# Reloading a residual in the layout of turned column tiles: four strided loads a tile, or an early DRAM-to-DRAM copy and one load

## The chip, the cores and the metric

The kernel runs on one core of one Trainium2 chip. The metric is device time in microseconds (us) of one execution, lower is better. In what follows PE is the matrix engine (PEld its weight loads), DVE the vector engine, ACT the scalar engine, POOL GpSimd, and SP the engine that here does nothing but issue transfers. SP and ACT each have a queue of transfers. All transfers are carried out by the same 16 DMA engines.

## The reference, cut to what matters

`x` has 3327 rows of 512 floats, `adj` is a 3327 x 3327 matrix, all in float32. There are two layers, each with a residual:

```python
# layer 0
h = maximum(layernorm(x), 0)
q, k, v = h @ Wq.T + bq, h @ Wk.T + bk, h @ Wv.T + bv
x = x + softmax(q @ k.T * scale + adj + adj) @ v
# layer 1
h = maximum(layernorm(x), 0)
A2 = adj + eye
dscale = diagonal(A2) ** -0.5
x = x + relu((dscale[:, None] * A2 * dscale[None, :]) @ (A2 @ h @ W.T))
```

The `x` between the two layers is called x1 in the kernel. It is computed in the middle of the program, and wanted again at the end, when `relu(...)` of layer 1 is added to it.

## The kernel before, in words

Rows are padded to 3328, which is 26 tiles of 128. They are split into two strips, `s = 0` and `s = 1`, each with two halves `y` of `HT[s]` = 7 or 6 row tiles, so `H[s]` is 896 or 768 rows. A first part computes the attention weights and leaves them in DRAM. Then come three big matrix products, numbered `g` = 0 (attention times h), 1 (A2 times h) and 2 (A2 times the result of 1 times W).

Each `g` is made of seven smaller products `ORDER = ("p5", "p1", "p6", "p7", "p2", "p3", "p4")` of a Strassen-like scheme, each for both strips, and each in seven **steps** (six pairs of row tiles and one single one). So one `g` has 7 x 2 x 7 = 98 steps. A step with a pair makes 14 matmul instructions at L918; a single one makes 8 at L909. `number_of(g, r, s, t)` is a step's number, and `run(k)` issues the program of step `k`.

Which work stands in which step is written out by hand: `at(k, what)` puts a function into the dictionary `between`, and the engines' instruction order is then fixed as traced (`in_order`, SP and DVE among them). In `run(k)` the order on SP is: the left tiles of step `k + 3` (`steps[k + 3].load()`, L832 and L836, two transfers of 448 or 384 KB into a ring of five slots, `a_ring`), then every function of `between[k]` that has "load" in its name, in the order in which it was registered. Those of the right-hand rows (`Right.load`, L856 and L870) are registered before the ones of this case. The sums that DVE makes of a left tile (`four_sums`, L163 to L165, behind L899 for a diagonal) are traced two steps ahead of the matmuls that use them, and DVE also combines finished products (`Gather`, L962 to L981).

The result of `g = 2` is held transposed, as column tiles `cts[s][y][d]` (128 features by `H[s]` rows). Twelve blocks at the very end are turned by PE (`turn_last`, `finish`). The other fourteen column tiles are handled by class `Columns`, one every three steps of the last three products: DVE turns the tile in 32 x 32 blocks (`turn`, L1145), scales it (`scale`, L1151), and adds x1 (`add`, L1154), and SP stores it to `out`, four transfers a tile (L1157, posted so that SP issues them two steps later). The x1 for this has to lie in the same block-turned layout. `load` (L1141) therefore fetches it from `x1d`, which is x1 row by row in DRAM, with four transfers of 32 partitions, whose contiguous runs are 32 floats or 128 bytes:

```python
rows = rows.rearrange("(j r) (c a e) -> c a r j e", r=32, a=4, e=32)
return [(tile[32 * a : 32 * a + 32].rearrange("r (j e) -> r j e", e=32), rows[self.d, a]) for a in range(4)]
```

The tile that receives it is one of two slots (`xp_slots`). The load is placed two steps ahead of `turn`, and four ahead of `add`. x1 itself is written by ACT's queue at the end of `g = 0` and in the beginning of `g = 1`, between 999 and 1218 us.

Of the kernel before, what the change touches and what calls it, by code (L numbers as in the profile page):

```python
# [10 lines left out]
F32 = mybir.dt.float32  # L11
# [4 lines left out]
P = 128  # L16
# [23 lines left out]
H = tuple(n * P for n in HT)  # L40
# [7 lines left out]
def graph_layers_kernel(  # L48
# [30 lines left out]
    nc = tc.nc  # L79
    NP, D = x.shape  # L80
    DC = D // P
# [13 lines left out]
    def half(k, shape, name):  # L95
        return arena.tile(shape, F32, name=name, tag=f"half{k}")
# [31 lines left out]
    dram = ctx.enter_context(tc.tile_pool(name="dram", bufs=1, space=bass.MemoryType.DRAM))  # L128
# [25 lines left out]
    pd = [[dram.tile([P, len(E_AT), H[s]], F32, name=f"p{s}_{t}") for t in range(HALF)] for s in range(2)]  # L154
    sumd = [[dram.tile([P, len(SUMS), H[s]], F32, name=f"sum{s}_{t}") for t in range(HALF)] for s in range(2)]
    x1d = [[dram.tile([HT[s] * P, D], F32, name=f"x1d{s}{y}") for y in range(2)] for s in range(2)]
    rowd = [[dram.tile([P, D], F32, name=f"row{g}_{i}") for i in range(NT)] for g in range(3)]
    normd = {k: [dram.tile([1, 2 * 4 * P], F32, name=f"norm{m}_{k}") for m in range(2)] for k in range(4)}
    t2d = [[dram.tile([P, 4, P], F32, name=f"t2{g}_{t}") for t in range(PAIRS + 1)] for g in range(3)]
# [157 lines left out]
    def after(ins, other):  # L317

        tc.add_manual_dep(ins.ins, other.ins.name,
                          mybir.DependencyInfo(mybir.DependencyClass.NoSync, mybir.DependencyReason.DATA),  # L320
                          reason="in_order")

    class Turned:
# [23 lines left out]
        def load(self):  # L347
            k, w = self.k, self.w
            self.other = half(2, [P, 2, BW], "a21")[:, :, :w]
            a11, a12, a22 = hp[k][:, 0], hp[k][:, 1], hp[k][:, 2]  # L350
            for y, blocks in enumerate(((a11, a12), (self.other, a22))):
                c0 = ROW[y * HALF + PACKS[k][0]] * P
                xs = xT[:, c0 : c0 + w].rearrange("(z c p) e -> z p c e", z=2, p=P)
                for z, to in enumerate(blocks):
                    after(nc.sync.dma_start(to, xs[z]), self.row)
            self.norms = []
            for m in range(2):
                self.norms.append(half(m, [P, 2, BW], "norms")[:, :, :w])
                self.loaded = nc.sync.dma_start(
                    self.norms[m], normd[k][m][0:1, : 2 * w].rearrange("a (y e) -> a y e", y=2).to_broadcast([P, 2, w]))  # L360
# [766 lines left out]
    class Columns:  # L1127
# [5 lines left out]
        def parts(self, tile, rows):  # L1133

            rows = rows.rearrange("(j r) (c a e) -> c a r j e", r=32, a=4, e=32)
            return [(tile[32 * a : 32 * a + 32].rearrange("r (j e) -> r j e", e=32), rows[self.d, a]) for a in range(4)]

        def load(self):
            self.x = next(xp_slots)()[:, : H[self.s]]
            for to, rows in self.parts(self.x, x1d[self.s][self.y]):  # L1140
                nc.sync.dma_start(to, rows)  # L1141

        def turn(self):
            self.o = turn_ring([P, H[0]], "turned")[:, : H[self.s]]
# [20 lines left out]
    def number_of(g, r, s, t):  # L1165
        return ((g * len(ORDER) + r) * 2 + s) * len(every) + t

    def at(k, what, *args):
        between.setdefault(k, []).append((what, args))
# [44 lines left out]
    for n, (s, y, d) in enumerate(((0, 1, 2), (0, 1, 3), (1, 1, 2), (1, 1, 3), (0, 0, 0), (0, 0, 1), (1, 0, 0),  # L1214
                                   (1, 0, 1), (0, 0, 2), (0, 0, 3), (1, 0, 2), (1, 0, 3), (0, 1, 0), (0, 1, 1))):
        part = Columns(s, y, d)
        for what, later in ((part.load, -2), (part.turn, 0), (part.scale, 1), (part.add, 2)):
            at(k + later, what)
        k += 3 if n < 12 else 2
    for n, i in enumerate(range(20, NT, 2)):  # L1220
        at(number_of(2, 6, 1, 2) + n, last_load, i)
# [494 lines left out]
```

## Time and profile before

| what | value |
|---|---|
| median of 3 runs | 2166.07 us (2165.14 to 2173.19) |
| the profiled execution's own time | 2169.72 us |
| its span from first to last instruction | 2167.9 us |
| PE busy | 2142.5 us (99%) |
| DVE busy | 1653.3 us (76%) |
| HBM read, written | 416.68 MB, 167.84 MB |
| DMA packets, those under 512 bytes | 400530, 139788 |
| the four loads of a tile, L1141 | 56 transfers of 112 or 96 KB, 1943.2 to 2135.2 us |
| the four stores of a tile, L1157 | 56 transfers, 1977.0 to 2156.1 us |

How to read it: times inside the profile count from the first instruction, so the profiled execution's 2169.72 us is its span and 1.8 us around it. PE is busy nearly always, so what counts is where it isn't. A row of the timeline or of the chain has a start, a duration, an engine and a line; a small q behind an engine's name means its sequencer, which waits and issues but doesn't compute. `a<-b` means that a is written from b. In a table of windows, each engine has its busy time and its number of instructions, then come the granted PE clock as a share, the mean busy share of the 16 DMA engines and what they moved in GB/s. That share adds the times of packets, which overlap, and can go above 1.

In this profile, the steps of `g = 2` begin at 1748 us, the last three products and with them the column tiles' loads at 1943 us.

### The profile page before, as it was taken

What the parts mean: (1) busy time and instruction counts of PE and PEld (TensorE: products, weight loads), DVE (VectorE), ACT (ScalarE), POOL (GpSimd) and SP (SyncE); (2) the same over time, 40 slices, a digit from 0 to 9 for tenths busy, and PEclk for the clock granted to TensorE, in tenths of its full rate; (3) what the DMA queues carried; (4) which work ended last, traced back from release to release, by engine and by line L of the source; (5) the groups of instructions that cost most, each with busy time, mean ns of one, the idle gap of its engine ahead of it and who ended that gap; (6) DMA issues with size and microseconds to landing.
All of it is one profiled execution on the core that took longest, in us unless ns stands there. A gap on an engine that the chain in (4) does not pass through costs nothing.

```text
span 2167.9 us, 20907 instructions
## 1 busy us (share of the span) xinstructions
PE 2142.5 (99%) x6272; PEld 1182.1 (55%) x6272; DVE 1653.3 (76%) x3235; ACT 273.1 (13%) x441; POOL 68.4 (3%) x63
## 2 busy tenths in 40 slices
PE   9999999999999999999999999999999999999997
PEld 5555555555555555555454555555666655555553
DVE  7479888888887688767777778886666568779886
ACT  5312211112110000001110000010111100000000
POOL 2000000000004000000111000000000000000000
PEclk9999999999999999999999999999999999999998
DMA  8678888888999899889797889886646368769997
GB/s 298 214 255 287 308 313 279 303 296 304 322 299 308 299 364 329 280 290 314 259 318 257 303 292 362 309 302 213 206 133 224 129 195 294 247 183 237 263 254 172
DMA packets 400530, 586.07 MB, mean 270 GB/s; under 512 B 139788, under 2 KB 273304, under 8 KB 400408
## 3 DMA queue, kind: packets, MB, share of 16 engines
q1 hardware_dynamic: 372472, 527.08, 74.5%
q10 hardware_dynamic: 27936, 57.56, 7.2%
q8 instruction: 52, 0.85, 0.2%
q14 instruction: 70, 0.57, 0.1%
HBM read 416.68 MB, written 167.84 MB: 270 GB/s over the span
## 4 chain that ended last, share of the span: by engine, by line
PE 90%; DVE 5%; DMA 3%; issue 1%; SPq 0%; POOL 0%; ACT 0%; DVEq 0%
PE p L918 52%; PE Y L541 13%; PE Z L541 6%; PE p L909 5%; PE p L1025 4%; PE pw L1086 3%; PE X L541 3%; PE Y L397 2%; PE Z L397 1%; DMA part<-in_adjT_dram 1%; DVE part L163 1%; DMA part<-p 1%; DMA rows<-row 0%; PE X L397 0%; DMA wk<-in_wk_dram 0%
## 5 line engine op out<-in xcount | busy, mean ns | idle before, releaser
L918 PE MATMUL p<-part,b 128*128 128x448 f32 (+1 forms) x3528 | 1261.2, 514 | 5.2 <-DVE part L962 4.0
L918 PEld LDWEIGHTS p<-part,b 128*128 128x128 f32 x3528 | 670.8, 190 | 549.4 <-issue 292.4
L163 DVE TENSOR_TENSOR part<-part 128x896 f32<-128x896 f32 (+1 forms) x252 | 257.0, 1020 | 79.0 <-DMA part<-sum 27.9
L541 PE MATMUL Y<-qt,hp 128*128 128x448 f32 (+1 forms) x832 | 308.2, 513 | 2.5 <-DVE g L553 1.6
L541 PEld LDWEIGHTS Y<-qt,hp 128*128 128x128 f32 x832 | 157.8, 190 | 136.2 <-issue 72.7
L541 PE MATMUL Z<-qt,hp 128*128 128x384 f32 (+1 forms) x416 | 162.2, 512 | 0.0
L165 DVE TENSOR_TENSOR part<-part,part 128x448 f32<-128x448 f32 (+1 forms) x219 | 129.5, 591 | 14.9
L164 DVE TENSOR_TENSOR part<-part,part 128x448 f32<-128x448 f32 (+1 forms) x219 | 129.4, 591 | 7.2
L909 PE MATMUL p<-part,b 128*128 128x448 f32 (+1 forms) x336 | 124.2, 512 | 0.0
L541 PEld LDWEIGHTS Z<-qt,hp 128*128 128x128 f32 x416 | 79.0, 190 | 66.2 <-issue 38.1
L545 DVE SCALAR_TENSOR_TENSOR g<-g,Y 128x384 f32<-128x384 f32 (+1 forms) x156 | 91.5, 586 | 29.7 <-PE Y L541 26.0
L961 ACT COPY part<-p 128x384 f32<-128x384 f32 (+1 forms) x33 | 16.6, 503 | 664.0 <-PE p L918 512.2
L909 PEld LDWEIGHTS p<-part,b 128*128 128x128 f32 x336 | 63.8, 190 | 54.1 <-issue 31.5
L548 ACT ACTIVATE g<-g 128x768 f32<-128x768 f32 (+1 forms) x48 | 43.0, 896 | 346.8 <-DVE g L545 286.9
L541 PE MATMUL X<-qt,hp 128*128 128x384 f32 (+1 forms) x208 | 81.1, 512 | 0.0
L962 DVE TENSOR_TENSOR part<-p,part 128x384 f32<-128x384 f32 (+1 forms) x33 | 19.3, 586 | 57.3 <-PE p L918 56.5
L1025 PE MATMUL p<-w,ct 128*128 128x512 f32 x136 | 61.6, 592 | 0.0
L541 PEld LDWEIGHTS X<-qt,hp 128*128 128x128 f32 x208 | 39.5, 190 | 33.1 <-issue 19.3
L981 DVE TENSOR_TENSOR ct<-p,part 128x448 f32<-128x448 f32 (+1 forms) x72 | 42.5, 609 | 18.2 <-PE p L909 13.8
L190 POOL TENSOR_TENSOR rstd<-ve,mhalf 128x1 f32<-128x1 f32 x46 | 38.7, 843 | 531.1 <-DVE ve L188 502.8
L1086 PE MATMUL pw<-w,rows 128*128 128x256 f32 x208 | 53.5, 380 | 0.4 <-DVE rows L1076 0.4
L1016 DVE TENSOR_TENSOR job<-job 128x896 f32<-128x896 f32 (+1 forms) x52 | 53.0, 1019 | 0.0
(194 smaller groups left out, 1683.2 us busy)
## 6 DMA issues: line engine op xcount, KB each, us to landing
part<-sum SPq DMA_DIRECT2D x104, 448.0 KB, 5.0
part<-p SPq DMA_DIRECT2D x91, 448.0 KB, 6.0
part<-sum SPq DMA_DIRECT2D x104, 384.0 KB, 3.8
part<-p SPq DMA_DIRECT2D x91, 384.0 KB, 4.6
part<-in_adjT_dram SPq DMA_DIRECT2D x78, 448.0 KB, 4.9
b<-row SPq DMA_DIRECT2D x234, 128.0 KB, 4.9
part<-in_adjT_dram SPq DMA_DIRECT2D x78, 384.0 KB, 3.7
g<-in_adjT_dram SPq DMA_DIRECT2D x52, 448.0 KB, 4.2
```

The costliest lines, as they stand in the source:

```text
L163: yield nc.vector.tensor_add(o[:, 0:2], g[:, 0:4:3], g[:, 1:2].to_broadcast([P, 2, g.shape[-1]]))
L164: yield nc.vector.tensor_add(o[:, 2], o[:, 1], g[:, 0])
L165: yield nc.vector.tensor_add(o[:, 3], o[:, 2], g[:, 2])
L397: nc.tensor.matmul(ps[:, :w], M[B[name]][:, c, o * P : (o + 1) * P], hp[k][:, A[name], c], start=start and c == 0, stop=c == 1, skip_group ...
L541: nc.tensor.matmul(ps[:, :wd], h_of(self.t, name, k), qt[B[name]][:, k], start=start and k == 0, stop=k == 1, skip_group_check=True)
L545: nc.vector.scalar_tensor_tensor(a[n], a[n], 2.0, ps[:, :wd], op0=ALU.mult, op1=ALU.add if sign > 0 else ALU.subtract)
L548: nc.scalar.activation(g[1], g[1], AF.Exp, **({"bias": pad} if self.t == HALF - 1 else {}))
L909: yield nc.tensor.matmul(ps[("p2", "p3", "p4", "p8")[k]][:, :w], b[:, z], a[:, 0, y], start=k == 3 and not self.seeded, stop=True, skip_gr ...
L918: yield nc.tensor.matmul(ps[r][:, :w], b[:, i], m, start=self.t == 0 and not adds, stop=self.t == PAIRS - 1 and r in ("p1", "p5", "p6", "p ...
L1016: nc.vector.tensor_add(self.a, self.a, self.b)
L1025: nc.tensor.matmul(ps, cts[s][y][d][:, k * P : (k + 1) * P], w[d], start=d == 0, stop=d == DC - 1)
L1086: nc.tensor.matmul(ps, a, W[B[name]][:, c], start=new and c == 0, stop=c == 1, skip_group_check=True)
```

## The change

x1 gets a second copy in DRAM, `x1c`, in the layout of the column tiles: for every `d`, 128 rows of `H[s]` contiguous floats. A new function `reload` writes a quarter of a tile into it, DRAM to DRAM, with one transfer on SP. Fourteen tiles make 56 quarters, which are put into steps 1 to 55 of `g = 2`, one a step (two in step 48), in the first four products. `load` then fetches a tile in one transfer. Its place in the order stays, and so do `turn`, `scale`, `add` and the stores. As "reload" has "load" in its name, `run(k)` issues it with the loads at the beginning of a step, behind those of the right-hand rows.

```diff
     x1d = [[dram.tile([HT[s] * P, D], F32, name=f"x1d{s}{y}") for y in range(2)] for s in range(2)]
+    x1c = [[dram.tile([DC, P, H[s]], F32, name=f"x1c{s}{y}") for y in range(2)] for s in range(2)]
...
+        def reload(self, a):
+
+            tile = x1c[self.s][self.y][self.d]
+            to, rows = self.parts(tile, x1d[self.s][self.y])[a]
+            nc.sync.dma_start(to, rows)
+
         def load(self):
             self.x = next(xp_slots)()[:, : H[self.s]]
-            for to, rows in self.parts(self.x, x1d[self.s][self.y]):
-                nc.sync.dma_start(to, rows)
+            nc.sync.dma_start(self.x, x1c[self.s][self.y][self.d])
...
         part = Columns(s, y, d)
         for what, later in ((part.load, -2), (part.turn, 0), (part.scale, 1), (part.add, 2)):
             at(k + later, what)
+        for a in range(4):
+            at(number_of(2, 0, 0, 0) + 1 + 4 * n + a - (n > 11), part.reload, a)
         k += 3 if n < 12 else 2
```

## The prediction

> **What bounds the kernel now.** The page comes first. PE is busy 2142.5 of 2167.9 us, so no change of transfers can bring more than PE's idle time and what a lowered clock costs it.
>
> ```profile
> PE 2142.5 (99%) x6272; PEld 1182.1 (55%) x6272; DVE 1653.3 (76%) x3235; ACT 273.1 (13%) x441; POOL 68.4 (3%) x63
> ```
>
> Second, the table of windows, for the two stages that the change touches (the first four products of g = 2, then the last three) and for the one place where PE stands still.
>
> ```profile
> 1748.00:1943.00 195.00, 195.00 (x561) 106.21 (x560) 146.20 (x274) 8.90 (x18) 0.00 (x0) 1.00 0.72 237
> 1943.00:2140.00 197.00, 192.25 (x542) 103.85 (x541) 163.08 (x280) 13.73 (x27) 0.00 (x0) 0.98 1.00 249
> 2107.50:2121.46 13.96, 9.21 (x24) 4.10 (x23) 7.12 (x10) 1.08 (x2) 0.00 (x0) 0.95 0.92 208
> 2121.46:2128.80 7.34, 7.34 (x14) 4.09 (x15) 7.19 (x13) 0.00 (x0) 0.00 (x0) 0.62 1.22 261
> ```
>
> The first stage has a full PE and a DMA share of 0.72. The second has a share of 1.00, and loses 4.75 us of PE, all of it after 2107.5. There the chain of waits leaves PE:
>
> ```profile
> 2081.87 20.31 PE p L918 x54
> 2102.18 0.51 SPq L836
> ...
> 2102.74 5.03 DMA part<-in_adjT_dram
> ...
> 2109.69 2.54 PE p L918 x6
> 2112.23 0.47 SPq L836
> ...
> 2112.80 5.74 DMA part<-in_adjT_dram
> ...
> 2121.46 15.26 PE p L918 x38
> ```
>
> Two left tiles come late, and behind each hang DVE's sums and then PE: 0.76 us at 2109 and 3.98 us at 2117.5 by the timeline of PE. Why they are late is in the timeline of SP (start, duration):
>
> ```profile
> 2088.95 6.50 SPq L1141 DMA_DIRECT2D part<-x1d  x4
> 2095.55 0.94 SPq L836 DMA_DIRECT2D part<-in_adjT_dram  x2
> ...
> 2097.49 4.58 SPq L1157 DMA_DIRECT2D out_dram<-turned  x4
> 2102.17 1.68 SPq L836 DMA_DIRECT2D part<-in_adjT_dram  x3
> 2103.95 8.18 SPq L1141 DMA_DIRECT2D part<-x1d  x4
> 2112.23 0.94 SPq L836 DMA_DIRECT2D part<-in_adjT_dram  x2
> ```
>
> SP hands out the left tiles the moment it is through with a column tile's four loads. It was inside those for 8.18 us, 5.3 of them a wait for an earlier x1d load to land (SP's own waits), while a slot of the left ring had long been free.
>
> **What the Trainium skill says.** "DMA: Bandwidth & Descriptors", section "Why small descriptors are slow (HBM only)": each packet has a fixed cost. The trace agrees: in 1973 to 1976 us nothing but 128-byte loads ran, 1420 packets at a share of 0.377, so 0.377 x 3 us x 16 / 1420 = **12.7 ns** each; in 2147 to 2151 nothing but 128-byte stores, 3536 at 0.719, **13.0 ns** each. Same page, "Issuing engines are not separate DMA queues": all queues share the 16 engines, so an early copy has to fit beside that stage's own traffic. Same page, "Latency and other measured facts", gives the only price of DRAM to DRAM: 207 to 214 GB/s for tiles of 16 KiB rows. 128 bytes at that rate are an estimated 16 x 128 / 207 = 9.9 ns of one engine, below the fixed cost. No transfer here goes from DRAM to DRAM, so the trace doesn't say. "TensorE: Matmul & The Clock Gate", section "What's actually happening": after an idle window of about 3.4 us the clock is halved. The trace agrees: after 3.98 us idle the next 7.34 us had a clock of 0.62.
>
> **The change part by part.**
>
> *Taken away in the last three products:* 56 loads with 8 x 3584 + 6 x 3072 = 47104 packets, 47104 x 13 ns / 16 = 38 us of the DMA engines; and on SP the time inside them. The five tiles from 2070 on cost SP 5.63 + 6.50 + 8.18 + 5.11 + 3.61 = 29.0 us by its timeline.
>
> *Put in their place:* 14 loads of 448 or 384 KB in rows of 3584 or 3072 bytes, the shape of the left tiles (an issue 0.5 us, landing 4 to 5 us). 6.03 MB at the 349 GB/s of the best 20 us (1820 to 1840) are 17 us. So the stage gets 38 - 17 = 21 us of DMA back, about a tenth, and SP about 26 us from 2070 on. The stores stay, four small ones a tile, about 4.5 us of SP each.
>
> *The path:* with SP ahead again, left tiles are issued when their slot is free. The first of the two was 0.93 us late for DVE, the second 6.1. PE gets back 0.76 + 3.98 us, and 14 matmuls that took 7.34 us at the lowered clock take 4.51 (84 of this width take 27.09 elsewhere in the chain), 2.83 less. Sum **-7.6 us**. Late next is DVE: in this product it has about 5.3 us of work in a step of 5.26 us (its L163 start at 2084.0, 2089.3 and 2094.65, back to back), so its lead before PE stays near nothing but doesn't turn negative; between 2111 and 2121 it has 6.1 us of idle time that goes too. From PE's last L909 matmul at 2154.1 to the end, 13.8 us of combining, turning and storing stay as they are. Nothing more is to be had between 1943 and 2100, where PE is full.
>
> *The two waits of DVE* at 2136 to 2143 (0.2 and 3.64 us) lie after that; they vanish behind PE, which bounds the end then. I count nothing for them.
>
> *Added in the first four products:* 56 copies on SP, one a step. Issue: L1141's median is 0.605 us, so 34 us; at the price inside a group of four (some 5 us / 4) 70 us. This is hidden, since SP waits there for PE to free slots, 62.2 + 52.5 us in SP's own waits. Behind a copy on SP stands only the next step's left tile, which has to wait for PE anyway.
>
> ```profile
> SPq L832 <- PE p L918: 62.2, 33, 4.6
> SPq L836 <- PE p L918: 52.5, 22, 4.9
> ```
>
> Carrying: 47104 packets. At 13 ns 38 us, which with 0.72 x 195 = 140 us make 178 of 195: it fits, 0.7 us a step. The tightest part, 1800 to 1840, has a share of 0.95 and would go to about 1.13, 5 us late at its end. What covers that: a left tile is issued when PE leaves the step five before its own, so it has four steps of 4.5 to 5.3 us, at least 18 us; landing takes 5, the sums 1.09 + 0.62 + 0.63 = 2.3, and DVE's block of combining some 4.6. About 6 us are left. Bounds of the unknown price: below, 10 ns (the estimate above) or 28 us, no gain on the path since PE is full there; above, both ends in DRAM could add up to 26 ns or twice that. Free time in the stage is 0.28 x 195 = 55 us, used up at 55 x 16 / 47104 = 19 ns; with the 6 us of cover at 21 ns. I take 13 ns, since loads and stores, with DRAM on different sides, cost the same. Cost 0, range 0 to 25 us.
>
> *Waits added:* a load waits for its tile's copies, which were issued at least 37 steps before (the last tile: copied in steps 52 to 55, loaded in 92), some 170 us. If the wait covers the whole `x1c[s][y]`, the first load, in step 54, waits for a copy of the step before, which lands meanwhile. Nothing.
>
> The profiled 2169.72 becomes 2162.1, -0.35%. It lay 3.65 us above the median; the same 7.6 us off the median of 2166.07 give 2158.5, said as **2159**. A measurement tells about 0.5% here, 10.8 us, from no change, so this likeliest case is "within".
>
> **The rivals.**
>
> *A, half the gain (the end turns out bound by DVE, or by the stores):* DVE is 9.76 of 10 us busy from 2080 on, and stores still make SP stand 4 to 5 us a tile. Then the second stall shrinks under the length that lowers the clock but stays: -3 to -5, **2162**. For it: leads of near nothing. Against: DVE idles 6.1 us on a transfer right there.
>
> *B, slower: DRAM to DRAM is dear.* Place: steps of p1 and p6, 1800 to 1860, then to 1943. It decides from 21 ns a packet on; at 30 ns the copies are 88 us, 88 - 55 - 6 = 27 us of PE stall, less 7.6, so +19, **2185**; shorter stalls also lower the clock. For it: no row shows the price, and short writes to DRAM may each read first. Against: 128-byte stores to DRAM take the same 13.0 ns as loads from it.
>
> *C, the change doesn't take the wait away:* the left tile is late because of the stores, and the loads' time just goes to them. **2166**. Against: SP's longest stay, 8.18 us, is in L1141.
>
> *D, more than asked:* the unprofiled runs stall more, or the tail of 13.8 us shortens by 3 us with the DMA engines free: **2153**.
>
> **How the numbers follow.** Main case 0.50 (own range 2155 to 2163), A 0.15, C 0.06, D 0.11, B 0.18. Faster by over 0.5% (under 2155.2): D and the lower edge of the main case, 0.15. Slower by over 0.5% (over 2176.9): nearly all of B, 0.17. Within: 0.68. The range leaves out the far ends of D and B: 2152 to 2179.
>
> **What would show it.** Right: PE without a gap over 0.3 us from 1943 until its last L909, clock 1.00 there, SP's L1141 at 14 issues of about 0.5 us, left tiles never waited for at 2118, packets under 512 bytes unchanged in number but moved to 1748 to 1943, whose DMA share goes to about 0.92. Wrong: PE gaps behind L163 between 1800 and 1943, left tiles there landing over 8 us after their issue, copies of over 20 ns a packet; or the stall at 2117 still there with SP in L1157.

## The result, and the profile after

The changed kernel takes 2159.2 us in the median of 6 runs (2156.64 to 2160.37), the kernel before 2167.32 us in 6 runs, the three of the table above among them. The ratio is **0.9959, with a 95% interval of 0.9946 to 0.9972**. That is 8 to 9 us faster, as forecast (2159). It is less than the 0.5% that the prediction took a measurement to tell, but the interval lies clear of 1. The profiled execution took 2159.13 us, its span is 2157.3 us.

Lines of kernel.py move with the change: L918 is L919, L836 is L837, L909 is L910, L1104 is L1105; the copy is L1143, the one load of a tile L1147, its stores L1163. From the page of the changed kernel, and from its table of windows for the two stages and the place of the old gap:

```profile
PE 2137.5 (99%) x6272; PEld 1180.9 (55%) x6272; DVE 1652.0 (77%) x3235; ACT 273.1 (13%) x441; POOL 68.1 (3%) x63
```

```profile
1748.00:1943.00 195.00, 195.00 (x560) 106.21 (x559) 145.80 (x272) 8.61 (x17) 0.00 (x0) 1.00 0.86 261
1943.00:2140.00 197.00, 197.00 (x566) 107.35 (x565) 168.08 (x288) 14.20 (x28) 0.00 (x0) 1.00 0.87 255
...
2107.00:2121.00 14.00, 14.00 (x41) 7.60 (x40) 11.46 (x19) 1.08 (x2) 0.00 (x0) 1.00 0.79 232
```

PE is full in both stages, at full clock. The DMA share went from 0.72 to 0.86 in the first and from 1.00 to 0.87 in the second. The chain of waits no longer leaves PE in the last product, until 5.8 us before its last matmul ends:

```profile
2080.48 31.57 PE p L919 x84
2112.05 3.01 PE p L910 x8
2115.06 23.88 PE p L919 x74
```

Where the 10.6 us of span come from, by comparing the two profiles: 1.4 us lie ahead of the last product (it starts at 2081.87 before, at 2080.48 after). They are there from the 81st matmul on (25.09 us before, 23.70 after), which the change doesn't touch; in the profiles of all kernels of this document it starts between 23.55 and 25.09. From the start of the last product's matmuls to the end of the last L909 or L910 it is 2154.12 - 2081.87 = 72.25 us before and 2144.73 - 2080.48 = 64.25 after, so **8.0 us**. The tail behind that went from 13.8 to 12.6 us.

One correction to what stands ahead of the prediction: the steps of g = 2 begin earlier than 1748 us, since the weight products stand in its first steps. The copies run from 1671.4 to 1946.4 us. Of the 56, 44 lie in the stage from 1748 to 1943, one behind it, and 11 ahead of it, where DMA had more room (the packets of queue q1 at 45.6% of 16 engines between 1671 and 1748, against 33.8% before).

The price of a copy's packet, which no row of before could show, follows from the tables of DMA queues for 1748 to 1943, before and after:

```profile
DMA packets 21991, 46.12 MB, mean 237 GB/s; under 512 B 2433, under 2 KB 9221, under 8 KB 21982
...
q1 hardware_dynamic: 20686, 43.78, 68.3%
```

```profile
DMA packets 58576, 50.87 MB, mean 261 GB/s; under 512 B 38976, under 2 KB 45760, under 8 KB 58567
...
q1 hardware_dynamic: 57271, 48.53, 83.0%
```

36543 more packets under 512 bytes took 14.7% of 195 us on 16 engines, so 0.147 x 195 us x 16 / 36543 = **12.6 ns** each. From DRAM to DRAM costs what the loads (12.7) and the stores (13.0) of this size cost.

### The profile page after: what moved, and what is told of

Its sections match the earlier page's. It is cut to its first block, busy times and chain, and to the rows that moved or that the text cites. A ratio compares the mean times of both kernels' runs of the same rounds, so it can differ in the third digit from the quotient of the medians.

```text
span 2157.3 us, 20906 instructions
## 1 busy us (share of the span) xinstructions
PE 2137.5 (99%) x6272; PEld 1180.9 (55%) x6272; DVE 1652.0 (77%) x3235; ACT 273.1 (13%) x441; POOL 68.1 (3%) x63
## 4 chain that ended last, share of the span: by engine, by line
PE 93%; DVE 4%; DMA 2%; issue 1%; POOL 0%; ACT 0%; SPq 0%; DVEq 0%
PE p L919 55%; PE Y L542 13%; PE Z L542 6%; PE p L910 5%; PE p L1026 4%; PE pw L1087 3%; PE X L542 3%; PE Y L398 2%; PE Z L398 1%; DMA rows<-row 1%; DMA part<-sum 1%; PE X L398 0%; DMA wk<-in_wk_dram 0%; DVE part L164 0%; DVE st L185 0%
## 5 line engine op out<-in xcount | busy, mean ns | idle before, releaser
L919 PE MATMUL p<-part,b 128*128 128x448 f32 (+1 forms) x3528 | 1257.6, 513 | 0.8 <-DVE part L165 0.6
L919 PEld LDWEIGHTS p<-part,b 128*128 128x128 f32 x3528 | 669.9, 190 | 542.1 <-issue 291.8
L165 DVE TENSOR_TENSOR part<-part,part 128x448 f32<-128x448 f32 (+1 forms) x219 | 129.4, 591 | 7.2
L910 PE MATMUL p<-part,b 128*128 128x448 f32 (+1 forms) x336 | 124.2, 512 | 0.0
L910 PEld LDWEIGHTS p<-part,b 128*128 128x128 f32 x336 | 63.8, 190 | 54.1 <-issue 31.0
L963 DVE TENSOR_TENSOR part<-p,part 128x384 f32<-128x384 f32 (+1 forms) x33 | 19.3, 585 | 62.2 <-PE p L919 61.4
```

Of the source, the lines that this page charges most:

```text
L165: yield nc.vector.tensor_add(o[:, 2], o[:, 1], g[:, 0])
L910: yield nc.tensor.matmul(ps[("p2", "p3", "p4", "p8")[k]][:, :w], b[:, z], a[:, 0, y], start=k == 3 and not self.seeded, stop=True, skip_gr ...
L919: yield nc.tensor.matmul(ps[r][:, :w], b[:, i], m, start=self.t == 0 and not adds, stop=self.t == PAIRS - 1 and r in ("p1", "p5", "p6", "p ...
```

## The experiments

Theory S is the prediction's: SP is held inside four strided loads, so left tiles are issued late. Theory D: the DMA engines are overloaded in the last products, and taking small packets out is what helps. Theory X came up on the way. A completion semaphore is the counter that tells that a transfer has landed. SP may only issue a transfer when the one that used its completion semaphore before has landed; the semaphores go round among the transfers of SP and ACT in program order; and ACT issues its six loads of x1 for the last twelve blocks (L1104) late, when PE lets it. The traces bear the first two parts out: they name the semaphore of every transfer, and eight of them serve SP and ACT together, in turn. All ratios are to the kernel before on the same chip, with 95% intervals.

### Are the copies hidden?

**Copies made, but not used.**

```diff
-            nc.sync.dma_start(self.x, x1c[self.s][self.y][self.d])
+            for to, rows in self.parts(self.x, x1d[self.s][self.y]):
+                nc.sync.dma_start(to, rows)
```

> The 56 copies are made as in the change, but the tiles are still loaded with four 128-byte-run transfers from the rows. Theory S (the gain is SP's: it is no longer held inside four loads, and the copies are hidden): as before, ratio 0.998 to 1.002, about 2167 us, with PE's gap of some 4 us near 2117 still there. Theory C (the copies cost something, and the change's gain is net of it): slower than before by that cost, 2 us or more, and PE gaps between 1670 and 1950.

Measured: 1.0013 (1.0001 to 1.0025). PE is busy 195.00 of 195 us in the stage of the copies. The gap after 2117 is there (5.43 us), and one of 1.01 us at 2085. So the copies stall nothing where they run, but without the one load they bring nothing. The small loss sits in the last product; why it is a little larger there than before was not settled.

**Each copy made twice, and three times**, the further ones into DRAM tiles that nobody reads.

```diff
             nc.sync.dma_start(to, rows)
+            for other in spare_x1:
+                nc.sync.dma_start(self.parts(other[self.s][self.y][self.d], x1d[self.s][self.y])[a][0], rows)
```

> The change, with every copy made twice, the second into a DRAM tile that nobody reads: 112 copies, 94208 packets, an estimated 76 us of the DMA engines, as if one copy had 25 ns a packet. The prediction's sum (55 us free in the stage and 6 us of cover) gives 76 - 61 = 15 us of PE stall: 2174 us, ratio to before 1.003. Rival: the cover is larger, since part of the copies lies ahead of the stage counted and packets' times overlap: no PE gap, 2159 us, ratio 0.996.

> The change with every copy made three times, two of them into DRAM tiles that nobody reads: 168 copies, 141312 packets. Twice cost about 8 us of PE time in the stage of the copies (gaps of 4.9 us in all and two drops of the clock), while the gap at 2117 was gone. If the free time of the DMA engines is used up by then, every further packet costs in full: 44 of 56 copies lie in the stage, 44/56 x 38 = 30 us more, 2190 to 2200 us, ratio 1.010 to 1.014. If SP's waits for completions rather than the engines' time are what stalls: less, 2175 to 2185 us, 1.003 to 1.008.

Measured: twice 0.9994 (0.9984 to 1.0004), 2168.37 us; three times 1.0198 (1.0182 to 1.0213), 2211.26 us. Windows of the two, the stage of the copies:

```profile
1748.00:1943.00 195.00, 190.09 (x529) 101.12 (x528) 138.59 (x258) 8.52 (x17) 0.00 (x0) 0.98 0.98 274
```

```profile
1748.00:1943.00 195.00, 168.61 (x445) 87.67 (x444) 114.82 (x223) 5.95 (x12) 0.00 (x0) 0.92 0.98 252
```

Against the changed kernel (2159.2) that is 9.2 and 52.1 us (by the ratios 7.6 and 52). Twice lies between the two expectations, three times beyond both. The prediction's sum, copies less 55 us of free DMA time and 6 of cover, gives 76 - 61 = 15 and 115 - 61 = 54. It is too dear by 6 us or more at twice. That it fits at three times is in part luck: it counts all copies as lying in the stage, and it counts no lowered clock. Up to the last product's end PE idles for 32.6 us there, and 25.3 us of its matmuls ran at half the clock, an estimated 13 us more; some 5 us were not settled. At a DMA share of 0.98 PE pays in both kernels: at three times DVE's sums wait 58.2 us for left tiles (L163 of before, L165 here; its waits from 1748 to 1980). One set of copies, at a share of 0.86, cost PE nothing.

### What holds SP?

**The four strided loads spread**, one a step, no copy.

```diff
-            for to, rows in self.parts(self.x, x1d[self.s][self.y]):
-                nc.sync.dma_start(to, rows)
+            self.load_part(0)
...
+        for a in range(1, 4):
+            at(k - 2 + a, part.load_part, a)
```

> No copy and no second layout: the four strided loads of a tile are issued one a step, in the steps k-2 to k+1, instead of four in step k-2. Packets, bytes and stage are those of before. Theory S (SP's burst is what makes left tiles late): as the change, about 2159 us, ratio 0.996, PE without a gap after 1700. Theory D (what counts is the 21 us of DMA time that the change takes out of the last three products): stays at about 2167 us, ratio 0.999 to 1.001, left tiles still late at 2117.

Measured: 1.0021 (1.0011 to 1.0030), slower. Timeline of PE (start, duration, what, idle time ahead of it and who ended it):

```profile
2080.21 2.73 PE L918 MATMUL p<-part,b 128*128 128x448 f32 x6 [0.59 <-DVE part L962]
2085.62 25.07 PE L918 MATMUL p<-part,b 128*128 128x448 f32 x66 [2.69 <-ACT p L955]
2111.58 4.78 PE L918 MATMUL p<-part,b 128*128 128x448 f32 x12 [0.88 <-DVE part L164]
...
2123.74 29.77 PE L918 MATMUL p<-part,b 128*128 128x384 f32 x84 [4.38 <-DVE part L962]
```

The gap near 2117 stayed, and gaps at 2080 to 2086 came. An issue now takes 0.43 us in the median instead of 0.605, all 56 together 32.7 us of SP instead of 59.8, and still nothing is gained. **Theory S falls in the form that the prediction gave it**: to break up the burst is not enough. As a part of the cause the burst isn't out, since the tie of theory X is in this kernel too: SP waits 6.0 us between its loads of 2105.26 and 2111.72 us, with ACT's six loads of x1 just ahead in the round of semaphores. Spread loads without that tie were not run.

**The four strided loads on ACT's queue.**

```diff
-                nc.sync.dma_start(to, rows)
+                nc.scalar.dma_start(to, rows)
```

> Before, with the four strided loads of a tile issued in one burst as before, but from ACT's queue instead of SP's. Packets, bytes and burst stay. Theory S: SP is free, so about 2159 to 2161 us, ratio 0.996 to 0.997; the share of DMA in the last three products stays about 1.00. Theory D: about 2167 us, ratio 1.000, since the DMA engines carry the same.

Measured: 0.9994 (0.9985 to 1.0003). The gap near 2117 is gone, but PE now stands 0.74 us at 2020, 1.06 us at 2083.5 and 2.69 us at 2088.9. Between 2070 and 2140 SP, which no longer issues these loads, waits 20.2 us for them to land, although what it issues then are other tiles:

```profile
SPq L836 <- DMA part<-x1d: 13.1, 3, 4.7
SPq L856 <- DMA part<-x1d: 6.0, 2, 4.5
...
SPq L870 <- DMA part<-x1d: 1.1, 1, 1.1
```

So a transfer that ACT issued holds up those of SP. This is where theory X comes from. It also means that SP was not freed by this edit, so it is no clean test of theory S.

**The copies late**, one a step, seven to four steps ahead of the tile's load.

```diff
-            at(number_of(2, 0, 0, 0) + 1 + 4 * n + a - (n > 11), part.reload, a)
+            at(k - 9 + a, part.reload, a)
```

> The change, with each tile's four copies made one a step in the steps k-9 to k-6, seven to four steps ahead of its load, so inside the last three products. SP issues there 5 transfers a tile, never in a burst of four loads, but the DMA engines carry the 38 us of small packets in that stage again, and the 17 us of long ones on top. Theory D (the DMA engines' time in the last three products decides): slower than before, ratio 1.003 or more, DMA share there above 1.0, PE gaps from 2060 on. Theory S (SP held by four loads in a row decides): like the change or little above, ratio 0.996 to 0.998. The spread loads have already spoken against S; here D would have to show a loss.

Measured: 1.0028 (1.0021 to 1.0036). PE stands at 2051, 2053, 2083, 2088, 2114 and 2126 us, 10.9 us in all. The DMA share from 1943 to 2140 is 0.97, not above 1.0 as expected. The early place of the copies is what makes the change a gain. That speaks for D, but this kernel also has one transfer a tile more on SP than before, so it doesn't tell D from X.

**Four long loads a tile**, from the early copy: the packets of the change, the number of transfers of before.

```diff
-            nc.sync.dma_start(self.x, x1c[self.s][self.y][self.d])
+            row = x1c[self.s][self.y][self.d]
+            for a in range(4):
+                nc.sync.dma_start(self.x[32 * a : 32 * a + 32], row[32 * a : 32 * a + 32])
```

> The change with its early copies, but each tile is loaded in four transfers of 32 partitions from the copy, in rows of 3584 or 3072 bytes, in one burst on SP. Theory D: the number of transfers is worth nothing, 2159 to 2160 us, ratio 0.996 as the change, each of the four issues about 0.4 us instead of the 1.4 of the short ones. Theory S (four transfers in a row on SP are what hurts): half or less of the gain, ratio 0.998 to 1.000.

Measured: 0.9992 (0.9985 to 0.9998). Nearly the whole gain is lost, though an issue takes only 0.413 us in the median and the small packets are gone. Timeline of PE and chain of waits:

```profile
2113.04 3.17 PE L910 MATMUL p<-part,b 128*128 128x448 f32 x8
2120.20 29.42 PE L919 MATMUL p<-part,b 128*128 128x384 f32 x84 [3.99 <-DVE part L963]
```

```profile
2109.51 2.19 DMA xr<-x1d
...
2111.78 0.35 SPq L837
...
2112.24 5.04 DMA part<-in_adjT_dram
...
2117.40 0.97 DVE part L164
```

This is the only gap from 1700 us on, and the chain names its cause: a load of x1 for the last blocks (`xr`, issued by ACT at 2109.5, right after a copy for which ACT had waited 25.41 us for PE) lands, only then may SP issue the left tile, and then come its landing, the sums and PE. SP's waits between 2095 and 2116, of this kernel and then of the changed one:

```profile
SPq L837 <- DMA xr<-x1d: 8.9, 1, 8.9
```

```profile
SPq L1163 <- DMA xr<-x1d: 10.9, 1, 10.9
```

The changed kernel has the same tie, and longer. But there it falls on a store (L1163), with the next left tile issued ahead of it, which the kernel before issued at 2112.23. SP's timeline of the changed kernel:

```profile
2098.13 0.89 SPq L837 DMA_DIRECT2D part<-in_adjT_dram  x2
2099.07 12.99 SPq L1163 DMA_DIRECT2D out_dram<-turned  x4
```

With three transfers more a tile it falls on the left tile (L837).

**The six late loads from SP instead of ACT**: in the kernel before, and in the one with four long loads.

```diff
-            nc.scalar.dma_start(xr[:, k], x1_of(i + k)[:, 0:E])
+            nc.sync.dma_start(xr[:, k], x1_of(i + k)[:, 0:E])
```

> Before, with the six loads of x1 for the last twelve blocks (L1104) issued from SP instead of ACT; nothing else. In the profiles of before and of the change SP waits from 2111 to 2115, or from 2099 to 2112, for those loads to land, because a transfer may only be issued when the one that used its completion semaphore before has landed, and ACT issues these six only when PE lets it, at 2109. Theory X (this tie is what makes the left tile of the stall at 2117 late): the gap of 4 us near 2117 goes, 2160 to 2162 us, ratio 0.997. Theory D: the gap stays or moves, ratio 0.999 to 1.001.

> The four long loads a tile (which lost the gain: PE gap of 3.99 us at 2120, behind a left tile for which SP had waited 8.9 us on a load of x1 issued by ACT), with those six loads of x1 issued from SP. Theory X (the shared completion semaphores tie SP to ACT's late loads, and the number of transfers decides which of SP's transfers meets the tie): the gap goes and the gain is back, 2159 to 2161 us, ratio 0.996. Theory N (four issues a tile are themselves too many for SP): stays at 0.999.

Measured: before with them 0.9980 (0.9972 to 0.9988), four long loads with them 0.9967 (0.9956 to 0.9979). Timelines of PE, the kernel before with them first:

```profile
2085.98 31.28 PE L918 MATMUL p<-part,b 128*128 128x448 f32 x78 [2.69 <-ACT p L955]
2117.09 3.17 PE L909 MATMUL p<-part,b 128*128 128x448 f32 x8
2120.10 1.45 PE L918 MATMUL p<-part,b 128*128 128x384 f32 x4
2121.76 0.91 PE L918 MATMUL p<-part,b 128*128 128x384 f32 x2 [0.21 <-DVE part L965]
2123.16 25.45 PE L918 MATMUL p<-part,b 128*128 128x384 f32 x78 [0.48 <-DVE ct L981]
```

```profile
2111.71 3.17 PE L910 MATMUL p<-part,b 128*128 128x448 f32 x8
2114.72 27.25 PE L919 MATMUL p<-part,b 128*128 128x384 f32 x84
```

With four long loads the gap of 3.99 us is gone and most of the gain is back: theory X is shown for that gap. In the kernel before, the same edit brings about half of the gain, less than expected. The 3.98 us at 2117 go there too, but the left tile hardly comes earlier. SP, which now waits for none of ACT's loads there, is still inside the four strided loads for 6.38 us, nearly all of it issuing, and the left tile goes out at 2112.06 us, against 2112.23 before (it lands at 2116.92 against 2118.53). SP's timeline:

```profile
2105.57 6.38 SPq L1141 DMA_DIRECT2D part<-x1d  x4
2112.06 1.00 SPq L836 DMA_DIRECT2D part<-in_adjT_dram  x2
```

The gap is small mostly because PE gets there 2.8 us later (its single step ends at 2120.26, against 2117.48): it has stood for 2.69 us at 2086, behind which its clock is at 0.50 for 3.4 us.

So by the times **two things had to go: the tie at 2112, and the strided loads of 128-byte runs**. Without the tie alone the ratio is 0.9980, without the strided loads alone 0.9992, without both 0.9967. The change does both: fewer transfers move the tie off the left tile, and the small packets go where there is room. Whether the strided loads hurt through SP's time in issuing them or through the DMA engines (share 1.00 from 1943 to 2140 with them and 0.93 without), no run separates.

### Where it is won, and a faster version

**Only the last seven, or only the first seven tiles** copied and loaded in one transfer, the others as before.

```diff
+        part.copied = n >= 7
```

> The change for the tiles 7 to 13 alone (loaded from 2040 us on); tiles 0 to 6 are loaded as before, and only 28 copies are made. If what counts is the DMA time in the last 80 us before the stall at 2117: all of the gain, 2159 us, ratio 0.996. If SP's or the DMA engines' backlog builds up from 1943 on: about half of it, ratio 0.998.

> The change for the tiles 0 to 6 alone (loaded up to 2040 us); tiles 7 to 13 as before, 28 copies. Copying the last seven alone gave all of the gain, so here none: 2167 to 2169 us, ratio 0.999 to 1.001, PE gaps at 2085 or 2117 as in the kernel before. If a backlog from 1943 on had a part: about 0.998.

Measured: last seven 0.9953 (0.9938 to 0.9969), 2159.36 us; first seven 0.9996 (0.9988 to 1.0004), with a gap of 4.89 us at 2118. The last seven give all of the gain that can be told, with half of the copies. A backlog from before 2040 us has no part that these runs show.

**All of it on SP**: the change, the six late loads and ACT's three last stores moved to SP.

```diff
-            finish(i, nc.scalar if n % 2 else nc.sync)
+            finish(i, nc.sync)
```

> The change, with the six loads of x1 for the last blocks and the three of six last stores that ACT issues moved to SP, so that no transfer of the last product is tied to another queue. PE is full until its last matmul already, so only the tail can move: SP's last stores, which wait 3.9 us for ACT's to land, could go 2 us earlier. 2156 to 2158 us, ratio 0.995; if the tail is not set by them, 2159 us as the change.

Measured: 0.9943 (0.9929 to 0.9956), 2156.61 us. From the last L910 to the end are 11.2 us (2146.5 to 2157.7), against 12.6 of the change. This is the fastest version in its median. Its interval overlaps that of the change, so a lead of some 2 to 3 us over it is not shown.

## Why the prediction was right, point by point

- **The sum on the path** was 0.76 + 3.98 + 2.83 = 7.6 us. The profile gives 8.0 for the same stretch. The clock's part came as counted: the 84 matmuls of the last strip went from 30.08 to 27.25 us, 2.83. Where the other 0.4 us of PE's time went was not settled. PE's timeline, before and then after:

```profile
2109.69 4.78 PE L918 MATMUL p<-part,b 128*128 128x448 f32 x12 [0.76 <-DVE part L164]
...
2121.46 30.08 PE L918 MATMUL p<-part,b 128*128 128x384 f32 x84 [3.98 <-DVE part L962]
```

```profile
2114.89 27.25 PE L919 MATMUL p<-part,b 128*128 128x384 f32 x84
```

- **DMA moved**: 21 us of the engines' time were to leave the last three products; the share fell by 0.13 of 197 us, 26. The copies' price of 13 ns was right (12.6), and with it rival B at 21 ns and more is out. The share of the first stage came out at 0.86 instead of some 0.92, as 44 of the 56 copies lie in it. The 61 us of room and cover that B's sum used were put too small, by 6 us or more at two copies, and fit at three only with luck, as said above.
- **SP in the stage of the copies**: its waits for PE in these two lines from 1748 to 1943 were 62.2 + 42.6 us (the prediction's 52.5 is from 1740 on), and fell to

```profile
SPq L837 <- PE p L919: 35.4, 18, 4.1
SPq L833 <- PE p L919: 29.4, 21, 4.1
SPq L833 <- DMA t<-b: 10.2, 3, 5.7
SPq L1143 <- DMA t<-b: 7.7, 1, 7.7
```

  so by 40 us, within the 34 to 70 given. The issues of the 44 copies took 24.8 us of them. Another part went to waits for stores of ACT (`t<-b`), 17.9 us after and 5.8 before. "Behind a copy stands only the next left tile" left that tie out. It is hidden here.
- **The step that fell short** is the reason given for the late left tile: "SP hands out the left tiles the moment it is through with a column tile's four loads". Of the 8.18 us in the loads ahead of the late tile, 6.6 were waits for landings, by SP's waits of before (2080 to 2140):

```profile
SPq L1141 <- DMA part<-x1d: 5.3, 1, 5.3
...
SPq L1141 <- DMA xr<-x1d: 1.3, 1, 1.3
```

  The prediction took the 5.3 us for the loads' own length, and read past the wait for `xr`, which ends at 2111.8. The semaphores in the trace show that both are the tie. The third load of this tile uses the semaphore of the first, because ACT's six loads of x1 and the second load lie between them in the round of eight; so it had to wait until the first, issued at 2103.95, had landed at 2110.22. The fourth uses that of the first `xr`, landed at 2111.81. Of the 29.0 us in the loads of the five tiles from 2070 on, 21.8 were issuing, so for the other tiles the reading holds. Spread loads, the loads moved to ACT, and four quick loads in their place all fail to bring the gain, which each of them should have brought on the prediction's reasoning; all three still meet shared semaphores. That one transfer a tile was enough rests on where the tie falls, which nothing in the prediction looked at. In this the right number was luck.
- **Rival C**, that the time would just go to the stores, was right in part: in the changed kernel SP does stand 12.99 us in L1163. The left tiles behind it came early enough for PE all the same. **Rival A** and DVE as the next bound didn't come: PE has no gap to its last L910. Of **rival D**'s shorter tail 1.2 us came.
- **The peak of 1800 to 1840** was put at a share of about 1.13 with the copies. It is 0.94 there: seven copies lie in it, while its other transfers are 1.4 MB less than before (11.8 of 13.2 MB). Nothing hung on it.

## What to carry to other kernels

When an issuing queue stands still, ask for each of its waits whose landing ended it and whether that transfer has anything to do with what is issued next: a transfer of another queue can hold it through a shared completion semaphore, and then the number and order of transfers decide what is late, not their bytes. Small-packet traffic is worth moving to a stage with room when its own stage is full, but price it first in the engines' time: here the same copy was free once, cost 8 to 9 us twice, and 52 three times. Try the parts of a change alone before crediting one: here half of the copies gave the whole gain, and four quick loads instead of one lost it.

## What the runs showed of the hardware that was not expected

- Copies from DRAM to DRAM in runs of 128 bytes cost 12.6 ns a packet and engine, no more than loads (12.7) or stores (13.0) in such runs.
- PE's clock fell after shorter idle times than the Trainium skill's page "TensorE: Matmul & The Clock Gate" (section "What's actually happening") has it, an idle window of about 3.4 us. With the copies made twice, a gap of 1.83 us, 0.31 us of idle time shortly ahead of it, was enough. Timeline of PE and windows of that kernel:

```profile
1851.17 0.99 PE L920 MATMUL p<-part,b 128*128 128x448 f32 x2 [0.31 <-DMA part<-sum]
1853.99 6.32 PE L920 MATMUL p<-part,b 128*128 128x448 f32 x12 [1.83 <-DVE part L166]
```

```profile
1853.70:1857.10 3.40, 3.11 (x4) 1.51 (x5) 1.62 (x4) 0.53 (x1) 0.00 (x0) 0.50 1.10 296
```

  The clock was at 0.50 for those 3.4 us, so this gap cost an estimated 1.83 + 3.4 / 2 = 3.5 us. Not every such gap does it: one of 2.69 us was followed by a clock of 0.50 with the six late loads on SP and with the strided loads on ACT, and left it at 1.00 with the spread loads and with the late copies. What decides, no run here shows.
